# Another order of head pairs, one ScalarE table for exp and log, experts' second products in the scores' banks, tail and first heads laid out anew

## The chip, the core and the metric

The kernel runs on one core of a Trainium2 chip. The core has a TensorE (PE, matmuls; its weight loads are shown apart as PEld), a VectorE (DVE), a ScalarE (ACT), a GpSimd (POOL) and a SyncE (SP), which here only issues DMAs. Each engine works through its own list of instructions in order and waits for others by semaphores. On-chip data lie in SBUF, matmul results in PSUM. The metric is the device time in microseconds (us) of one execution, the median of several runs.

## The reference, cut to what matters

```python
x = layernorm(x + attn1(x)); x = layernorm(x + ffn(x))      # x: (2, 1024, 256) fp32

def attn1(x):                                # one head of width 256, causal, pre-norm
    xn = layernorm(x) * gamma + beta
    q, k, v = xn @ Wq, xn @ Wk, xn @ Wv      # 256 x 256 each
    return softmax(causal(q @ k.T / 16)) @ v @ o_proj + x

def ffn(x):
    a = layernorm(x) * ln1_w + ln1_b
    q, k, v = a @ wq + bq, a @ wk + bk, a @ wv + bv   # 16 heads of 128
    q, k = rope(q), rope(k)
    h = x + (softmax(causal(q @ k.T / sqrt(128))) @ v) @ wo + bo
    t = layernorm(h) * ln2_w + ln2_b
    w = top2_of_4(softmax(t @ w_gate))       # two weights a token, softmax over the two
    m = sum_e w[:, e] * (gelu(t @ we1[e] + be1[e]) @ we2[e] + be2[e])   # all 4 experts computed
    return h + m
```

## The kernel before, in words

All data are fp32. A batch `b` (0 or 1) has 1024 tokens: 8 rows `i` of 128 tokens, in two halves `j` of four rows. The program order is written out by hand: a list `steps` with one step for each row of work (16 rows of the first attention, then 8 rows for each of 32 *units*), and fillers hung on the steps with `at`, `mid`, `end_of`, `first`, `late`. `spread` hands a list of pieces to consecutive steps, so many a step. Step 16 is `A0`; unit number k has the steps 16+8k to 23+8k. Each engine sees its part of this order, so the order decides what waits behind what.

A **unit** is one head of one batch, `(g, b, hh)`: head group `g` (0 to 7) has two heads `hh`, and a *pair* `(g, b)` is two units in a row. `pairs` (L810) sets their order: in the version before, group by group with batch 0 and then 1; the last four pairs run batch 0 of groups 6 and 7, then batch 1 of both.

For each row of a unit (`RowB`): `scores` (L716) multiplies queries and keys into a two-bank PSUM tile `sc` (two such tiles), DVE masks (L329) and takes the negated row maximum (L331), ACT takes exp with the row's sum (L336). What follows has two forms:

- *blocks*: ACT scales the row by 1/sum (L730), DVE transposes it in 32 x 32 blocks (L741) into `pair_sb` (half j=0) or into the space of `x1` (half j=1), and once four rows are there, `gather` (L765) puts the blocks in place by 16 DMAs of the SP queue, in two lots of 8, one step apart. The tile gathered into is `pT`.
- otherwise DVE scales the row (L732), PE transposes it (L348), and ACT and DVE move it to `pT` (L353, L351).

`U0, U1` say which units use blocks: before, from unit 1 on, except the last two units' first halves. `output` (L786) then multiplies `pT` with the values into `av`, so many steps (the *lag*, in `PARTS`) after the half's last row: with the default lags 8 (j=0) and 8, 9, 10 (j=1), given others for the last units; ACT moves `av` to `aT` (L802). When a pair is done, `b_output` (L668, L678) multiplies `aT` with `wo` and adds it to the hidden state `h` (tile `hx`).

Keys, queries and values of the next pair are made while the pair before it runs: `seven_products` (L570 and L561) makes a 2 x 2 block product with seven products and sums of blocks; the sums of weight blocks are `weight_sums` on POOL (L537-L540), those of tokens `x_sums` on DVE (L547, four a batch, once), ACT moves parts (L593, L595), DVE adds (L603). The first two units' keys and queries are made whole, by `b_project` (L506, L513). Each finished 512-column piece of keys or queries is then rotated: two SP DMAs swap its halves into `rot`, which has two buffers (L480, L481), and POOL does three operations (L485-L487, the *rope*), popped from `rope_later` a step later. For the keys of the second pair, DVE did the first of the three (`HELP`). `load_weights` brings a group's weights, from the SP queue if `g` is not 0 and from POOL's if it is; `scale_queries` scales wq on POOL (L472).

PSUM: two score tiles of two banks, two banks `acc` (`acc_tile`, in turn), two banks `tr` for transposes and `av`.

The layernorms take mean and variance by `ln_stats`; 1/std was a Sqrt on ACT and a reciprocal on DVE. exp, Sqrt and Gelu lie in different ACT tables, so between them ACT loads a table (ACT_TABLE_LOAD).

After the attention follow, for each half of each batch: norm (`m_norm`, to `xn`), `m_transposed`, `gate_products`, `gate` and `gate_best` (softmax and the two largest, on DVE with an exp on ACT), `m_bias` (be2 weighted, on DVE, L1177), and for each expert `hidden` (L1190, `acc` banks, Gelu on ACT) and `expert` (L1214, second product; L1223, weighted and added to `h` on DVE). `m_residual` adds `x1`, kept in DRAM meanwhile, on POOL; `o_stats` and `o_finish` normalise and store. The batch-0 part begins beside the last units, which are of batch 1; the rest is a list of calls after the last step (`end` = 272), in which the last half's `output(END)` and the last `b_output` stand too.

Of the kernel before, what the change touches and what calls it, by code (L numbers as in the profile page):

```python
# [12 lines left out]
F32 = mybir.dt.float32  # L13
# [5 lines left out]
P = 128  # L19
# [3 lines left out]
ROPE_THETA = 10000.0  # L23


@with_exitstack
def kernel(
# [117 lines left out]
    eps_t = const.tile([P, 2], F32, name="eps_t")  # L145
    nc.vector.memset(eps_t[:, 0:1], EPS)
    nc.vector.memset(eps_t[:, 1:2], EPS / 4)
    warm = const.tile([P, 1], F32, name="warm")
    nc.scalar.activation(warm, eps_t[:, 0:1], AF.Sqrt)
# [49 lines left out]
    def ln_rstd(var, n, eps):  # L199

        std = small.tile([P, NT], F32, tag="std", name="std")
        nc.scalar.activation(std[:, :n], var, AF.Sqrt, bias=eps)
        rstd = small.tile([P, NT], F32, tag="rstd", name="rstd")
        nc.vector.reciprocal(rstd[:, :n], std[:, :n])
        return rstd

    def ln_apply(dst, src, mean, rstd):
        nc.vector.tensor_scalar(dst, src, mean, rstd, ALU.subtract, ALU.mult)  # L208
# [60 lines left out]
    def a_stats(b, tiles):  # L269
        for k in tiles:  # L270
            ln_stats(mv_x[b], k, x1[:, b * NT + k, :])
        cs = slice(tiles[0], tiles[-1] + 1)
        nc.scalar.activation(
            rstd_x[b][:, cs], mv_x[b][:, cs, 1], AF.Sqrt, bias=eps_t[:, 0:1]
        )

    def a_rstd(b, tiles):
        cs = slice(tiles[0], tiles[-1] + 1)
        nc.vector.reciprocal(rstd_x[b][:, cs], rstd_x[b][:, cs])
# [127 lines left out]
    def a_finish(b, j):  # L407
# [10 lines left out]
        nc.scalar.activation(r, v, AF.Sqrt)  # L418
        rr[b, j] = r

    def a_rfinish(b, j):
        r = rr[b, j]
        nc.vector.reciprocal(r, r)
# [67 lines left out]
    HELP = ("wk",)  # L491
# [172 lines left out]
    def b_output(g, b, tiles):  # L664
# [18 lines left out]
    U0, U1, GP = 1, (NU - 2, NU), 2  # L683
# [4 lines left out]
        (NU - 3, 0): {7: range(0, 4)},  # L688
        (NU - 3, 1): {9: range(0, 8)},
        (NU - 2, 1): {7: range(0, 8)},  # L690
# [5 lines left out]
    class RowB:  # L696
# [36 lines left out]

        def transpose(self):
# [10 lines left out]
            if i % 4 == 0:  # L745
                pTs[self.u, j] = work.tile(
                    [P, 4 * (j + 1), 512], F32, tag=f"pT{j}", name="pT", bufs=1
                )
# [5 lines left out]
        def gather(self, part):  # L754
# [3 lines left out]
            if part == 0:  # L758
                pTs[self.u, j] = work.tile([P, n, 512], F32, tag=f"pT{j}", name="pT", bufs=1)
# [50 lines left out]
    pairs = [(g, b) for g in range(G - 2) for b in range(B)]  # L810
# [29 lines left out]

    ROWS0 = (2, 2, 2, 2, 2, 2, 2, 0)
# [7 lines left out]
    a_rstd(0, J0)  # L849
# [7 lines left out]
    a_rstd(0, J1)  # L857
# [10 lines left out]
    a_rstd(1, ALL)  # L868
# [34 lines left out]
    for k, (name, n) in enumerate((("wk", 0), ("wq", 0), ("wk", 1), ("wq", 1))):  # L903
        at(13 + k // 2, b_project, units[0], name, n)
    at(15, b_value, 0, 0, 0)
# [14 lines left out]
    for r, (name, n) in enumerate((("wk", 0), ("wq", 0), ("wk", 1), ("wq", 1))):  # L920
        at(A0 + 2 + r, b_project, units[1], name, n)
    at(A0 + 6, lambda: weight_sums("wk"))
    at(A0 + 6, lambda: weight_sums("wq"))
    at(A0 + 7, lambda: weight_sums("wv"))
    for n in range(2):
        at(A0 + 7, x_sums, 1, n)
        at(A0 + 8, x_sums, 1, 2 + n)
    for n in range(4):
        at(A0 + 18 + n, x_sums, 0, n)
    for k, (g, b) in enumerate(pairs):  # L930
# [9 lines left out]
        if k + 1 < len(pairs):  # L940
# [3 lines left out]
            if ng != g:  # L944

                before = s0 - NT + (6 if k == 1 else 0)
                at(before, load_weights, ng, ("wk",))
                at(before + (1 if k == 1 else 4), weight_sums, "wk")
# [13 lines left out]
        else:  # L962
            spread(s1, keys + queries, (2, 2, 2, 2, 2, 2, 2, 0))
# [93 lines left out]

    def m_stats(b, tiles):
        for k in tiles:
            ln_stats(mv_h[b], k, h[:, b * NT + k, :])  # L1060

    def m_sqrt(b, tiles):
        cs = slice(tiles[0], tiles[-1] + 1)
        nc.scalar.activation(
            rstd_h[b][:, cs], mv_h[b][:, cs, 1], AF.Sqrt, bias=eps_t[:, 0:1]
        )

    def m_rstd(b, tiles):
        cs = slice(tiles[0], tiles[-1] + 1)
        nc.vector.reciprocal(rstd_h[b][:, cs], rstd_h[b][:, cs])  # L1070

    def m_norm(b, j):

        xn = xn_tile()
        for k in range(4):
            i = 4 * j + k
            ht = h[:, b * NT + i, :]
            ln_apply(xn[:, k, :], ht, mv_h[b][:, i, 0:1], rstd_h[b][:, i : i + 1])
# [45 lines left out]
    def gate(b):  # L1124
# [5 lines left out]
        raw = t3("raw_g")  # L1130
        nc.scalar.activation(raw, lg, AF.Exp)
        raws[b] = raw

    def gate_best(b, n):
# [19 lines left out]
        if n:  # L1154
            e2 = t2("e2")
            nc.vector.tensor_tensor(e2, v, found[b, 0][0], ALU.subtract)
            nc.scalar.activation(e2, e2, AF.Exp)
# [26 lines left out]
    def hidden(b, j, e):  # L1184
        k0 = b * NT + 4 * j
        hT = bpool.tile([P, IC, 512], F32, tag=("Twq", "Twk")[e % 2], name="hT", bufs=BUFS[("wq", "wk")[e % 2]])
        for m in range(IC):
# [10 lines left out]
            nc.scalar.activation(hT[:, m, :], ph, AF.Gelu, bias=par[:, bcol : bcol + 1])  # L1198
        hTs[b, j, e] = hT

    turn, attention_done = [0], []

    def expert(b, j, slots):

        for n0 in range(0, len(slots), 2):
            two = slots[n0 : n0 + 2]
            turn[0] ^= 1
            if turn[0] and attention_done:
# [25 lines left out]
    def o_finish(b, j, ks):  # L1234

        tiles = [4 * j + k for k in ks]
        m_rstd(b, tiles)
        n = len(ks)
        o = xn_tile()
        for k in ks:  # L1240
            i = 4 * j + k
            ln_apply(
                o[:, k - ks[0], :], h[:, b * NT + i, :], mv_h[b][:, i, 0:1], rstd_h[b][:, i : i + 1]
            )
        dst = out[b, ds(tiles[0] * P, n * P), :].rearrange("(n p) d -> p n d", p=P)
        nc.sync.dma_start(dst, o[:, :n, :])
# [3 lines left out]
    at(s, m_stats, 0, J0)  # L1250
    at(s + 2, m_stats, 0, J1)
    at(s + 2, m_sqrt, 0, ALL)
    at(s + 3, m_rstd, 0, ALL)
    at(s + 3, m_norm, 0, 0)
    at(s + 4, m_norm, 0, 1)
    s += NT
# [146 lines left out]
```

## Time and profile before

| | us |
|---|---|
| median of 3 runs (lowest to highest) | 1213.24 (1212.55 to 1214.63) |
| the profiled execution, its time | 1212.0 |
| its span, first to last instruction | 1210.2 |
| PE busy / DVE / ACT / POOL | 1158.6 / 782.1 / 652.0 / 587.1 |
| PE busy in 30 to 60 us, of 30 | 30.00 |
| PE busy in 150 to 200 us, of 50 | 41.65 |
| PE busy in 800 to 1000 us, of 200 | 197.61 |
| PE busy in 1000 to 1150 us, of 150 | 135.91 |
| SP's queue moved | 144.78 MB |

How to read it: busy time is the sum of an engine's instructions, matmul ends are modelled, and PE's rows overlap a little. In rows of single instructions the columns are start, duration, engine, line, operation, output <- inputs, shape and count; "[2.03 <-DVE pr L732]" is the idle time before it and what ended it. In the list of waits the three numbers are the sum, the times and the longest. "clock" is the share of full speed that PE was granted.

### The profile page before, as it was taken

Reading aid. Unit: us, or ns where it says so; the run is one execution under the profiler, and the core shown is the slowest. Engines: PE = TensorE matmul, PEld = TensorE weight load, DVE = VectorE, ACT = ScalarE, POOL = GpSimd, SP = SyncE. Lnnn points to the kernel's source line nnn. Section 1 sums busy time; section 2 is a strip of 40 time slices with the busy share of each in tenths; the row PEclk is TensorE's granted clock in tenths of the full one; section 3 lists DMA queues with packets and bytes.
Section 4 is the critical chain, followed back from the end, with each engine's and each line's share of the span. In section 5 each row is a group of like instructions: output and inputs, shape, how many; then the busy total and the mean of one; then the engine's idle time right before and its main releaser. Section 6 shows DMA issues by size and latency. Waiting matters only on the chain.

```text
span 1210.2 us, 15511 instructions
## 1 busy us (share of the span) xinstructions
PE 1158.6 (96%) x4410; PEld 727.3 (60%) x4410; DVE 782.1 (65%) x1798; ACT 652.0 (54%) x1197; POOL 587.1 (49%) x577
## 2 busy tenths in 40 slices
PE   7999977989999999999999999999999998998997
PEld 5676644565656565666656565756565655655665
DVE  5555767656666666666576666666666667774576
ACT  3344445646565655656565656565655555442423
POOL 4005377655664647474837465665757572003000
PEclk9999999999999999999999999999999999999999
DMA  5001125776666666676666776777767775313001
GB/s 180 1 1 35 61 66 127 166 148 152 162 161 158 156 165 161 145 167 155 159 145 158 167 162 158 168 170 167 171 159 173 171 166 135 79 35 104 18 18 35
DMA packets 239765, 153.81 MB, mean 127 GB/s; under 512 B 20828, under 2 KB 221600, under 8 KB 239168
## 3 DMA queue, kind: packets, MB, share of 16 engines
q1 hardware_dynamic: 236576, 144.78, 51.2%
q0 software_dynamic: 1728, 4.89, 1.3%
q10 hardware_dynamic: 1376, 3.15, 0.7%
q8 instruction: 36, 0.59, 0.2%
q14 instruction: 49, 0.40, 0.1%
HBM read 19.57 MB, written 4.19 MB: 20 GB/s over the span
## 4 chain that ended last, share of the span: by engine, by line
PE 74%; SPq 8%; DVE 7%; DMA 5%; POOL 4%; issue 2%; ACT 1%; POOLq 0%; DVEq 0%; ACTq 0%
PE av L786 18%; PE sc L716 14%; PE pa L570 8%; SPq L765 7%; PE pa L668 6%; PE pa L561 5%; PE pa L1190 4%; PE pc L570 3%; DMA pT<-x 3%; PE sc L370 3%; PE pa L392 2%; PE pc L561 2%; PE pe L1214 1%; PE pa L1214 1%; DVE pair_sb L208 1%
## 5 line engine op out<-in xcount | busy, mean ns | idle before, releaser
L716 PE MATMUL sc<-Twk,Twq 128*128 128x512 f32 (+3 forms) x768 | 290.1, 486 | 0.7 <-POOL Twq L487 0.7
L786 PE MATMUL av<-pT,vg 128*128 128x512 f32 (+3 forms) x768 | 272.1, 493 | 18.7 <-DMA pT<-x 8.8
L730 ACT ACTIVATE pr<-pr,rs 128x640 f32<-128x640 f32 (+1 forms) x240 | 187.7, 782 | 179.4 <-DVE rs L728 179.2
L336 ACT ACTIVATE pr<-sc,nmx 128x128 f32<-128x128 f32 (+7 forms) x272 | 201.0, 739 | 153.4 <-DVE nmx L331 121.0
L786 PEld LDWEIGHTS av<-pT,vg 128*128 128x128 f32 x768 | 143.3, 191 | 140.2 <-issue 102.5
L716 PEld LDWEIGHTS sc<-Twk,Twq 128*128 128x128 f32 x768 | 140.0, 190 | 122.1 <-issue 107.1
L331 DVE TENSOR_REDUCE nmx<-sc 128x1 f32<-128x128 f32 (+7 forms) x272 | 206.1, 758 | 9.4
L329 DVE TENSOR_TENSOR sc<-sc,limit 128x128 f32<-128x128 f32 x272 | 79.6, 293 | 145.0 <-PE sc L716 130.0
L485 POOL TENSOR_TENSOR Twk<-Twk,rope_sb 128x512 f32<-128x512 f32 x60 | 76.4, 1273 | 199.2 <-DMA rot<-Twk 175.7
L486 POOL TENSOR_TENSOR rot<-rot,rope_sb 128x512 f32<-128x512 f32 x128 | 165.5, 1293 | 5.1 <-DMA rot<-Twk 5.1
L741 DVE STREAM_TRANSPOSE x<-pr 128x640 f32<-128x640 f32 (+1 forms) x124 | 128.8, 1039 | 54.4 <-DMA pT<-x 32.0
L668 PE MATMUL pa<-wo_g,aT 128*128 128x256 f32 x512 | 126.5, 380 | 2.1 <-DVE hx L678 1.0
L668 PEld LDWEIGHTS pa<-wo_g,aT 128*128 128x128 f32 x512 | 96.1, 191 | 38.1 <-issue 19.2
L485 POOL TENSOR_TENSOR Twq<-Twq,rope_sb 128x512 f32<-128x512 f32 x64 | 81.5, 1273 | 46.0 <-DMA rot<-Twq 27.3
L487 POOL TENSOR_TENSOR Twk<-Twk,rot 128x512 f32<-128x512 f32 x64 | 81.5, 1273 | 7.4 <-DVE Twk L485 2.5
L487 POOL TENSOR_TENSOR Twq<-Twq,rot 128x512 f32<-128x512 f32 x64 | 81.6, 1276 | 5.0
L678 DVE TENSOR_TENSOR hx<-hx,pa 128x256 f32<-128x256 f32 (+1 forms) x124 | 52.3, 425 | 31.2 <-PE pa L668 29.1
L802 ACT ACTIVATE aT<-av,par 128x512 f32<-128x512 f32 x64 | 43.9, 686 | 46.1 <-PE av L786 46.1
L1190 PE MATMUL pa<-xT,we_sb 128*128 128x512 f32 x128 | 59.4, 603 | 4.8 <-DVE hx L1223 4.8
L595 ACT ACTIVATE part<-pa,par 128x512 f32<-128x512 f32 x62 | 42.6, 687 | 39.5 <-PE pa L570 39.4
L741 DVE STREAM_TRANSPOSE pair_sb<-pr 128x128 f32<-128x128 f32 (+1 forms) x116 | 58.2, 502 | 3.6 <-issue 3.4
L447 POOL TENSOR_TENSOR hx<-x,bo_sb 128x256 f32<-128x256 f32 x16 | 12.2, 763 | 99.5 <-ACT x L444 99.5
(194 smaller groups left out, 1589.5 us busy)
## 6 DMA issues: line engine op xcount, KB each, us to landing
pT<-x SPq DMA_DIRECT2D x496, 128.0 KB, 2.6
pT<-pair_sb SPq DMA_DIRECT2D x464, 64.0 KB, 2.0
rot<-Twk SPq DMA_DIRECT2D x128, 128.0 KB, 2.3
rot<-Twq SPq DMA_DIRECT2D x128, 128.0 KB, 2.4
wk_g<-in_L_ffn_wk_dram SPq DMA_DIRECT2D x9, 256.0 KB, 3.1
wq_g<-in_L_ffn_wq_dram SPq DMA_DIRECT2D x9, 256.0 KB, 3.2
wv_g<-in_L_ffn_wv_dram SPq DMA_DIRECT2D x9, 256.0 KB, 3.0
wo_g<-in_L_ffn_wo_dram SPq DMA_DIRECT2D x9, 256.0 KB, 2.9
```

Source lines behind the costliest of these rows:

```text
L331: nc.vector.tensor_reduce(nmx, sc[:, :L], AX.X, ALU.max, negate=True)
L336: nc.scalar.activation(pr[:, :L], sc[:, :L], AF.Exp, bias=nmx, accum_out=sm)
L485: eng.tensor_tensor(t[:, cs], t[:, cs], rope_sb[:, 0, cs], ALU.mult)
L486: nc.gpsimd.tensor_tensor(rot, rot, rope_sb[:, 1, cs], ALU.mult)
L487: nc.gpsimd.tensor_tensor(t[:, cs], t[:, cs], rot, ALU.add)
L570: nc.tensor.matmul(pa, lhsT=w, rhs=x, start=start, stop=True, skip_group_check=True)
L668: nc.tensor.matmul(pa[:, ts(k, D)], lhsT=aT[g, b][:, hh, ts(i, P)], rhs=wg["wo"][:, hh, :], start=(hh == 0), stop=(hh == GH - 1),)
L716: nc.tensor.matmul(sc[:, ds(n0, n)], lhsT=qT[:, ts(i, P)], rhs=kT[:, ds(n0, n)], start=True, stop=True,)
L730: nc.scalar.activation(self.pr[:, :L], self.pr[:, :L], AF.Copy, scale=rs)
L741: nc.vector.transpose(z[:, i % 4, :n, :], self.pr[:, : n * 32].rearrange("p (m s) -> p m s", s=32))
L786: nc.tensor.matmul(cut(av), lhsT=vg[g, b][:, c, ts(hh, HD)], rhs=cut(pT[:, c, :]), start=(c == 0), stop=(c == i),)
L1190: nc.tensor.matmul(ph, lhsT=we1_sb[:, e, c, ts(m, P)], rhs=x2T[:, c, ds(k0 * P, 512)], start=(c == 0), stop=(c == DC - 1),)
```

## The change

The diff makes these edits:

1. Order of pairs: `(0,0), (1,0), (1,1), (0,1)`, then groups 2 to 5 with both batches each, then the last four as before. Group 0's weights are loaded a second time.
2. First heads: unit 1's keys and queries at steps 15 and 16 (were 18 to 21); the second pair's keys in unit 0 from its row 3 on, its queries in unit 1, one each step; group 1's weights and sums accordingly; `x_sums` of batch 0 at steps 14, 14, 15, 19 and of batch 1 at 24 to 27 (were batch 1 at 23 and 24, batch 0 at 34 to 37). `HELP` is empty.
3. One table: `ln_rstd` takes 1/std as exp(-0.5 ln(var)) on ACT; `TABLE`, which holds both, is loaded at the start, and again by `table()` before such an operation when a Gelu has been between. The reciprocals go.
4. Tail of attention: unit 30's first half uses blocks; units 29 and 30 use the default lags or 8 and 9; the last unit's first `pT` lies in a `vg` buffer. Batch 0's norm runs on POOL into free key and query buffers; statistics, norm, transposes, gate products and gate stand at other steps.
5. Experts: `expert` with four slots puts all four results in one score tile; with two slots it takes a score tile or an `acc` bank in turn.
6. After the last step: another order of calls; `o_finish` normalises on ACT (Identity with scale and bias) and stores from the ACT queue.

```diff
-    HELP = ("wk",)
+    HELP = ()
+    def ln_rstd(rstd, var, eps=0.0):
+        nc.scalar.activation(rstd, var, AF.Ln, bias=eps)
+        nc.scalar.activation(rstd, rstd, AF.Exp, scale=-0.5)
...
-    U0, U1, GP = 1, (NU - 2, NU), 2
+    U0, U1, GP = 1, (NU - 1, NU), 2
     PARTS = {
...
-        (NU - 3, 0): {7: range(0, 4)},
-        (NU - 3, 1): {9: range(0, 8)},
-        (NU - 2, 1): {7: range(0, 8)},
+        (NU - 2, 1): {8: range(0, 4), 9: range(4, 8)},
         (NU - 1, 0): {4: range(0, 4)},
         (NU - 1, 1): {END: range(0, 8)},
...
-    pairs = [(g, b) for g in range(G - 2) for b in range(B)]
+    pairs = [(0, 0), (1, 0), (1, 1), (0, 1)]
+    pairs += [(g, b) for g in range(2, G - 2) for b in range(B)]
     pairs += [(g, b) for b in range(B) for g in (G - 2, G - 1)]
...
+    XS0 = (14, 14, 15, A0 + 3)
+    XS1 = (A0 + 8, A0 + 9, A0 + 10, A0 + 11)
...
+    for k, (name, n) in enumerate((("wk", 0), ("wk", 1), ("wq", 0), ("wq", 1))):
+        at(A0 - 1 + k // 2, b_project, units[1], name, n)
-    for r, (name, n) in enumerate((("wk", 0), ("wq", 0), ("wk", 1), ("wq", 1))):
-        at(A0 + 2 + r, b_project, units[1], name, n)
...
-                before = s0 - NT + (6 if k == 1 else 0)
+                before = s0 - NT if k else s0
                 at(before, load_weights, ng, ("wk",))
-                at(before + (1 if k == 1 else 4), weight_sums, "wk")
+                at(before + (4 if k else 3), weight_sums, "wk")
...
-            spread(s1, keys + queries, (2, 2, 2, 2, 2, 2, 2, 0))
+            spread(s0, keys, (0, 0, 0, 1, 1, 2, 2, 1))
+            spread(s1, queries, (1, 1, 1, 1, 1, 1, 1, 0))
...
+    def table():
+        if other:
+            nc.scalar.preload_act_table_set(TABLE)
+            other.clear()
...
+    def m_norm(b, j, eng=nc.gpsimd):
+        if b:
+            xn = xn_tile()
+        else:
+            xn = bpool.tile([P, 4, D], F32, tag=("Twk", "Twq")[j], name="xn", bufs=BUFS[("wk", "wq")[j]])
...
-        for n0 in range(0, len(slots), 2):
-            two = slots[n0 : n0 + 2]
-            turn[0] ^= 1
-            if turn[0] and attention_done:
+        for n0 in range(0, len(slots), 4):
+            two = slots[n0 : n0 + 4]
+            if len(two) > 2 or slots[0][1] % 2:
                 pe = ps_sc.tile([P, S], F32, tag="sc", name="pe")
             else:
                 pe = acc_tile()
...
+        nc.vector.scalar_tensor_tensor(
+            nb[:, :n], mv_h[b][:, cs, 0], -1.0, rstd_h[b][:, cs], ALU.mult, ALU.mult
+        )
...
+            nc.scalar.activation(
+                o[:, n0, :], h[:, b * NT + i, :], AF.Identity,
+                bias=nb[:, n0 : n0 + 1], scale=rstd_h[b][:, i : i + 1],
+            )
...
-        nc.sync.dma_start(dst, o[:, :n, :])
+        nc.scalar.dma_start(dst, o[:, :n, :])
```

The steps of the tail, counted from unit 30's first (256), before and after: statistics 0 and 2 in both; norm 3 and 4, now 1 and 3; transposes 4 to 7, now 5 to 8; gate products 6 to 9, now 9, 9, 10, 11; first `hidden` 6, now 8; `gate` 9, now 11; `gate_best` 10 and 11, now 11 and 12; `gate_weights` 12, now 13. After the last step the order of batch 0's second half and batch 1's preparation is now:

```diff
     all_of(0, 0, 2)
+    hidden(0, 1, 0)
+    gate_products(1, (0, 1))
+    gate_products(1, (2, 3))
+    all_of(0, 0, 3)
     steps[end - 1][0].output(END)
-    hidden(0, 1, 0)
+    m_bias(0, (6, 7))
+    hidden(0, 1, 1)
     for i in (4, 6):
         b_output(G - 1, 1, (i, i + 1))
...
     m_stats(1, J1)
...
+    all_of(0, 1, 0)
+    o_stats(0, 0, J0)
+    hidden(0, 1, 2)
+    m_rstd(1, J1)
+    m_rstd(0, J0)
+    m_norm(1, 1, nc.vector)
+    all_of(0, 1, 1)
+    m_residual(1, J1)
     for c in range(DC):
         m_transposed(1, 1, c)
```

Batch 1's first norm and its transposes stand before `all_of(0, 0, 2)`.

## The prediction

> **What bounds the kernel now.** I read the shares of the page first, then the busy time by stretch, then TensorE's (PE's) waits, then single rows around each wait.
>
> ```profile
> span 1210.2 us, 15511 instructions
> PE 1158.6 (96%) x4410; PEld 727.3 (60%) x4410; DVE 782.1 (65%) x1798; ACT 652.0 (54%) x1197; POOL 587.1 (49%) x577
> ```
>
> ```profile
> 60.00:90.00 30.00, 30.00 (x145) 23.07 (x144) 15.54 (x46) 14.24 (x28) 2.17 (x3) 1.00 0.00 1
> ...
> 150.00:200.00 50.00, 41.65 (x158) 22.98 (x156) 36.21 (x68) 28.36 (x55) 36.98 (x36) 1.00 0.30 79
> ...
> 600.00:800.00 200.00, 199.96 (x769) 123.72 (x768) 133.94 (x290) 122.96 (x232) 112.54 (x104) 1.00 0.68 158
> ...
> 1100.00:1125.00 25.00, 21.67 (x83) 14.29 (x82) 11.97 (x26) 9.14 (x11) 11.41 (x16) 0.93 0.08 35
> ```
>
> The columns are stretch, length, then busy time of PE, PEld, DVE, ACT and POOL, granted clock, DMA share, GB/s. PE is the bound: in the middle (600 to 800 us) it idles 0.04 us in 200, so nothing done there to DVE, ACT or POOL can bring time. What can be won is PE's 51.6 us of idle (1210.2 - 1158.6) and some clock, and both lie at the ends:
>
> ```profile
> PE av L786 <- DMA pT<-x: 8.8, 6, 3.7
> PE av L786 <- DMA pT<-pair_sb: 8.0, 3, 4.1
> PE pt L348 <- DVE pr L732: 5.4, 3, 2.5
> ...
> PE pa L1190 <- DVE hx L1223: 4.8, 3, 2.0
> ```
>
> Idle by place, from PE's rows: start 6.8; **A**, 143 to 169 us, 9.4 (2.03+0.85+0.68+0.26+1.49+2.52+1.55); **B**, 193 to 208, 6.5 (0.70+1.69+4.11); **C**, at 255, 3.7; changes of head group at 310 to 600, some 2.6; **D**, last attention rows, 930 to 1025, 6.6 (0.50+0.57+1.31+3.31+0.87); **E**, 1049 and 1071, 2.0 (1.04+0.96); **F**, experts, 7.8 (1.52+1.64+0.48+0.40+0.40+2.02+1.30); after the last matmul 6.1. A long wait costs twice, since the matmuls behind it run slowly:
>
> ```profile
> 207.61 4.08 PE L786 MATMUL av<-pT,vg 128*128 128x512 f32 x8 [4.11 <-DMA pT<-pair_sb]
> ...
> 230.70 2.32 PE L786 MATMUL av<-pT,vg 128*128 128x512 f32 x8
> ```
>
> The same eight matmuls take 4.08 us after the wait, 2.32 without it. The granted clock is 0.83 over 207 to 217, 0.94 and 0.89 over 247 to 267, 0.97 and 0.86 over 1110 to 1130: 1.7 us each behind B, C and F (shortfall times 10 us).
>
> **Order of pairs and first heads (A, B, C).** Unit 1's projections move from steps 18-21 to 15-16, the next pair's keys from unit 1 to unit 0, its queries stay in unit 1, one each step. PE's work is the same. POOL's ropes (3 x 1.27 us a tile) start where POOL now idles 12.0 us (127 to 139.5), so its queue at 190 to 197 goes. That queue makes B:
>
> ```profile
> 195.85 1.27 POOL L487 TENSOR_TENSOR Twq<-Twq,rot 128x512 f32<-128x512 f32 x1
> ...
> 197.12 0.53 SPq L480 DMA_DIRECT2D rot<-Twq  x1
> ...
> 200.20 5.59 SPq L765 DMA_DIRECT2D pT<-pair_sb  x8
> ```
>
> SP's next rotation waits for one of two rot buffers, which POOL frees at 197.1; the second half of unit 1's gather is queued behind it and lands as PE continues at 207.6. Afterwards unit 1 carries 4 tiles' rotations (8 DMAs) instead of 8 (16), and the wk and wq loads leave SP's queue there too: SP saves 8 x 0.57 + 2 x 0.53 = 5.6 us, more than the 4.11. The wait for ACT's part (1.69), itself behind late DVE rows, I keep at 0.7. B: 6.5 + 1.7 - 0.7 = **-7.5** (0 to -8.2).
>
> A is DVE: 9.83 busy of 10 us in 140 to 150 and 160 to 170. It loses four x_sums of batch 1 (1.61+1.64+0.78+0.94 = 5.0) and a reciprocal (0.2), gains one x_sum of batch 0 (0.68 to 1.61, take 1.0) and net two key sums (1.4): -2.8. With fewer ropes beside it the rest shortens too (two L208 take 2.78 us there, four take 1.38 at 14.6 us). The two normalising applies and row sums stay. Ends 0 and -9.4; I take **-5**.
>
> C stays: the gather of unit 2 shares the DMA engines with the 1 MB we1 load (step 40, landing 9.3 us), and in the compiled order POOL issues group 0's wk just ahead of it instead of wv on SP. **0** (+3 to -5.4).
>
> The order 0,1,1,0,2 loads group 0 a second time: four DMAs, which go through POOL because g is 0. Behind each on POOL queue the ropes, behind these SP's rotations and gathers; each waits until PE has read the old tile. Here a rule speaks against the change. The row: the first four such loads took 0.70 to 0.72 us of POOL each, with DVE working, and landed in 6.1 to 6.2 us, against 2.9 to 3.2 through SP. The Trainium skill, "SBUF — State Buffer", the box on DVE blocking DMA, says that a POOL-issued DMA cannot write its descriptors while DVE holds the shared port: about 3.1 us instead of 0.62. By the row the loads cost POOL 2.9 us over four units, by the rule 12.4. POOL idles about 12 us of a 28 us unit (44% in 600 to 800), so either is hidden; I take the row, and **+0.7** for one more change of group (a wait of 0.84 us at 371, behind a pT<-x gather; ends 0 and 3).
>
> **One table.** The page and the compiled order give 30 table loads before and 18 after; Sqrt plus DVE reciprocal becomes Ln plus Exp (0.30 us each, as the Sqrt).
>
> ```profile
> L1198 ACT ACT_TABLE_LOAD x9 | 11.5, 1283 | 14.0 <-PE pa L1190 13.9
> L336 ACT ACT_TABLE_LOAD x8 | 10.3, 1283 | 8.2 <-DVE nmx L331 6.0 <-DVE lg L1108 2.1
> L1064 ACT ACT_TABLE_LOAD x6 | 7.7, 1283 | 0.1
> ```
>
> By the row that is 12 x 1.28 = 15.4 us of ACT. The Trainium skill, "ScalarE: Activation LUTs", What ACT_TABLE_LOAD costs, adds a drain of 1.38 us and gives 2.66: 31.9 us. In this trace an exp ends at 1137.92, the load starts at 1137.94 and the next Gelu at 1139.23: no drain shows, and I take 1.28. Of either sum almost nothing is on the path, for ACT is 54% busy: at 137.5 to 140.8 two loads delay an exp while DVE is busy anyway. **0** of its own.
>
> **Tail.** D: batch 0's norm goes to POOL and to tiles of its own (8 x about 0.75, half of L472's 1.49 for 512 columns), two steps ahead of its transposes, while POOL idles from 1004 on. So pair_sb is free for the gathers of unit 30's first half: 16 more gathers on SP (10.5 us, no rotations are left then), and 10 PE transposes fewer at 0.107 (eight take 0.86): **-1.1**. Unit 29's first half is read at lag 8 instead of 7, about 3 us later, against a wait of 3.31. Of D's 6.6 the 2.4 of 936, 965 and 995 stay, and of the rest I leave 1.2: **-3.0** (+1 to -6).
>
> E: the output products now follow four more av matmuls (2.15 us), which hide ACT's aT (0.96 goes). But gate and its first best stand in one step, with a table load (1.28) and exp between them on ACT: DVE waits some 2 us, then the hidden-state adds, then PE. I take +1.3: **+0.3** (-1 to +3).
>
> F: experts' second products leave the two acc banks to hidden, and take two score tiles of two banks. The waits of 1.52, 2.02 and 1.30 were hidden's first product behind L1223 on a DVE busy with m_bias (4.0 us) or L208 (5.1). Unit 31's last av, now some 10 us later, gives its gather (landing 1095.4) time; batch 1's second norm has 10 us of products before its transposes. Late next is DVE itself (four L1223 take 1.7 us of 6.9 a round) and ACT in a round with two table loads, Ln, Exp and four Identity (0.61 each, the L444 row): 2.6+0.6+2.4+1.4 = 7.0 us against 6.9. I leave 1.5 of 7.8 + 1.7: **-8.0** (+2 to -9.5).
>
> End: DVE loses reciprocal and apply (0.54 a tile), so the last L1223, which starts 0.8 behind PE's end (1204.1) now, starts 0.4 earlier; ACT then has Ln, Exp, one tile's Identity and its DMA issue (0.4) before the last Identity, 2.1 us instead of 1.0: **+0.7**.
>
> Sum: -7.5 - 5 + 0 + 0.7 + 0 - 1.1 - 3.0 + 0.3 - 8.0 + 0.7 = -22.9. The profiled execution took 1212.0 us (span 1210.2 and 1.8 around it): 1189.1. The median of the runs is 1.2 above it, so **1190**.
>
> **Rivals.**
> 1. *Tail only moves its waits* (DVE and ACT late in F, POOL late in D): D, E and F bring nothing, 1190 + 11 = 1201. For it: ACT's 7.0 against 6.9. Against: the freed banks. 0.14.
> 2. *First heads stay bound by DVE and SP*: A and B bring nothing, 1190 + 12.5 = 1202. For it: A's applies stay. Against: POOL's idle 12 us. 0.12.
> 3. *More goes*: C (5.4) and the rest of A (4.4) too: 1180. 0.17.
> 4. *The change does little*: new waits eat all, 1212. 0.03.
> 5. *Slower: POOL's queue.* A group 0 load blocks POOL until PE has passed and the ropes behind it miss their step. Each time SP's gather is late as in B: 4.11 + 1.7 = 5.8 us, four times 23.2, and C grows by 3: 1216. It decides from a POOL delay above its 12 us of slack a unit. 0.05.
>
> The forecast itself, 1184 to 1197: 0.49. A measurement of this kernel tells 0.2% from nothing, 1210.8 to 1215.7. Range **1179 to 1203**, rivals 1 to 3 mostly inside. Faster 0.92, same 0.03, slower 0.05.
>
> **What would show it.** B right: no PE wait on pT<-pair_sb near 200 us and a clock near 1.00 there. A: DVE below 9 of 10 us at 140 to 170. C: a PE wait on pT<-x of 3 to 4 us near 245. F: no PE wait on L1223, clock 1.00 to the last matmul. E: a wait on L678 of over 1 us beside gate. Wrong: POOL waiting on PE at its weight loads, or PE idle in 250 to 450.

## The result, and the profile after

The changed kernel takes 1197.2 us (median of 4 runs, 1195.82 to 1197.69) against 1212.99 for the kernel before on the same chip (4 runs, 1212.55 to 1214.63). The ratio is 0.9866, with a 95% interval of 0.9848 to 0.9883. The profiled execution took 1197.6 us with a span of 1195.8. The forecast was 1190 with a range of 1179 to 1203: the sign and the range held. Profile to profile (1212.0 to 1197.6) the saving was 14.4 us, where the sum had 22.9.

The first lines of the page after:

```profile
span 1195.8 us, 15503 instructions
...
PE 1153.4 (96%) x4400; PEld 725.9 (61%) x4400; DVE 768.7 (64%) x1760; ACT 649.8 (54%) x1221; POOL 607.1 (51%) x594
```

PE's idle time went from 51.6 us to 42.4. The busy time by stretch (length, then PE, PEld, DVE, ACT, POOL, granted clock, DMA share, GB/s) for the places A, B, C, D and F of the prediction:

```profile
140.00:150.00 10.00, 8.56 (x38) 5.72 (x38) 6.86 (x19) 3.60 (x11) 3.21 (x6) 1.00 0.00 0
160.00:170.00 10.00, 8.69 (x43) 5.22 (x42) 7.82 (x15) 6.23 (x13) 8.75 (x8) 1.00 0.33 76
200.00:210.00 10.00, 7.53 (x30) 4.36 (x29) 4.09 (x11) 4.54 (x9) 1.48 (x2) 1.00 0.75 172
250.00:260.00 10.00, 10.00 (x44) 6.83 (x43) 5.95 (x13) 4.82 (x8) 8.26 (x8) 0.83 0.49 117
1020.00:1030.00 10.00, 9.29 (x23) 4.53 (x24) 5.61 (x11) 5.56 (x9) 0.00 (x0) 0.83 0.30 72
1120.00:1130.00 10.00, 9.19 (x45) 6.61 (x45) 5.84 (x20) 4.95 (x6) 2.50 (x4) 1.00 0.00 0
```

DVE is below 9 of 10 us in both stretches of A (it was 9.83 in each). The clock is 1.00 behind B and F. It is still 0.83 behind C, and it is now 0.83 in 1020 to 1030, where it was 1.00. PE's rows with the waits that remain:

```profile
149.73 0.52 PE L338 MATMUL pt<-ident,pr 128*128 128x128 f32 x3 [1.44 <-DVE pr L719]
...
172.43 5.83 PE L777 MATMUL av<-pT,vg 128*128 128x512 f32 x16 [1.21 <-DVE rs L715]
...
197.54 1.13 PE L550 MATMUL pc<-S,xT 128*128 128x128 f32 x8 [1.72 <-ACT part L582]
...
202.94 2.39 PE L777 MATMUL av<-pT,vg 128*128 128x512 f32 x8 [2.47 <-DMA pT<-pair_sb]
...
249.01 2.81 PE L777 MATMUL av<-pT,vg 128*128 128x512 f32 x4 [3.58 <-DMA rot<-Twq]
...
932.12 1.95 PE L777 MATMUL av<-pT,vg 128*128 128x512 f32 x4 [1.73 <-DMA rot<-Twq]
...
1003.74 2.40 PE L777 MATMUL av<-pT,vg 128*128 128x512 f32 x8 [0.65 <-DMA pT<-pair_sb]
...
1020.71 3.10 PE L777 MATMUL av<-pT,vg 128*128 128x512 f32 x4 [4.61 <-DMA pT<-pair_sb]
...
1120.55 0.33 PE L210 MATMUL pt<-ident,pair_sb 128*128 128x128 f32 x1 [0.41 <-DVE pair_sb L204]
```

At 249.01 and 932.12 the profile names a rotation; the same reads in b_lag and d_swap wait for their gathers (pT<-x). The row at 1020.71 is new: 4.61 us of idling, and the four matmuls behind it take 3.10 us where four take 1.88 at full clock (row 1020.59 of the run d_gather below). The places in one table, PE's idle time and lost clock together, against the prediction's terms:

| place | before | after | change | forecast |
|---|---|---|---|---|
| A, 120 to 187 us | 9.4 | 5.8 | -3.6 | -5 |
| B, 189 to 208 | 8.2 | 5.2 | -3.0 | -7.5 |
| C, near 250 | 5.4 | 5.3 | -0.1 | 0 |
| changes of group | 2.6 | 3.0 | +0.4 | +0.7 |
| **D**, 930 to 1025 | 6.6 | 10.6 | **+4.0** | **-3.0** |
| E | 2.0 | 1.4 | -0.6 | +0.3 |
| F, experts | 9.5 | 0.8 | -8.7 | -8.0 |
| PE transposes saved | | | -1.1 | -1.1 |
| after the last matmul | 6.1 | 6.5 | +0.4 | +0.7 |

These add up to -12.3. The other 2.1 us of the 14.4 lie in PE's busy time and in no place that I could name: it fell by 5.2 us, of which the saved transposes and the clock make 2.8. Of D's +4.0, 1.2 is the wait at 932 (0.50 before, 1.73 now); in the runs below that leave this place alone it lies between under 0.25 (d_late) and 1.49 (d_load), so it may be chance. The table (edit 3) has no place of its own, and has a run of its own below.

### The profile page after: what moved, and what is told of

Same layout as the page of the kernel before. It is cut to its first block, busy times and chain, and to the rows that moved or that the text cites. A ratio compares the mean times of both kernels' runs of the same rounds, so it can differ in the third digit from the quotient of the medians.

```text
span 1195.8 us, 15503 instructions
## 1 busy us (share of the span) xinstructions
PE 1153.4 (96%) x4400; PEld 725.9 (61%) x4400; DVE 768.7 (64%) x1760; ACT 649.8 (54%) x1221; POOL 607.1 (51%) x594
## 4 chain that ended last, share of the span: by engine, by line
PE 76%; SPq 7%; POOL 5%; DMA 5%; DVE 4%; issue 2%; ACT 1%; POOLq 0%; ACTq 0%; DVEq 0%
PE av L777 18%; PE sc L703 14%; PE pa L559 8%; PE pa L657 6%; SPq L756 6%; PE pa L550 5%; PE pa L1187 5%; PE pe L1210 4%; PE pc L559 3%; PE sc L360 3%; PE pa L382 2%; PE pc L550 2%; POOL rot L475 2%; DMA rot<-Twq 1%; POOL Twk L476 1%
## 5 line engine op out<-in xcount | busy, mean ns | idle before, releaser
L474 POOL TENSOR_TENSOR Twk<-Twk,rope_sb 128x512 f32<-128x512 f32 x64 | 82.0, 1280 | 201.2 <-DMA rot<-Twk 154.9
L657 PEld LDWEIGHTS pa<-wo_g,aT 128*128 128x128 f32 x512 | 96.3, 191 | 35.2 <-issue 18.5
L1079 POOL TENSOR_TENSOR hx<-hx,x 128x256 f32<-128x256 f32 x16 | 12.7, 827 | 96.8 <-DVE hx L1219 84.6
```

The source lines that it names most:

```text
L474: eng.tensor_tensor(t[:, cs], t[:, cs], rope_sb[:, 0, cs], ALU.mult)
L657: nc.tensor.matmul(pa[:, ts(k, D)], lhsT=aT[g, b][:, hh, ts(i, P)], rhs=wg["wo"][:, hh, :], start=(hh == 0), stop=(hh == GH - 1),)
```

## The experiments

Each kernel ran on the same chip as the kernel before, which took 1214.7 to 1215.1 us there (median), so ratios are compared, not times. Runs of one kernel lay up to 9 us apart, and the ratios' intervals are 0.2 to 0.9% wide. What a part is worth is therefore read from its place in the profile first, and from the ratio second. One of the runs (d_late) left D, and all before it, as in the changed kernel, and got 0.9849 against that kernel's 0.9866: ratios that differ by this little are not told apart. Of the runs that alter the changed kernel, only best is told apart from it by the ratio.

### D: who makes unit 29's second half late?

The new wait is for the second half of unit 29. SP's queue there (start, time taken by all, line, operation, how many):

```profile
1002.57 11.28 SPq L756 DMA_DIRECT2D pT<-x  x16
1013.96 12.46 SPq L756 DMA_DIRECT2D pT<-pair_sb  x16
```

The first row is unit 29's gather, the second the new one of unit 30. In the same stretch POOL loads 768 KB (issued at 1011.7 and 1012.5 us), and PE reads from lag 8 on, not at 9. The suspects were these three, and a fourth, that PE had lost work ahead of the read.

**d_lag**

```diff
     PARTS = {
...
+        (NU - 3, 1): {9: range(0, 8)},
         (NU - 2, 1): {8: range(0, 4), 9: range(4, 8)},
```

> The changed kernel with one row of the read plan put back: the second half of unit 29 is read whole at lag 9 again, not in parts from lag 8. Theory 1, the lag: TensorE simply asks a step too early, and the wait of 4.61 us at 1020.7 us shrinks by the work of a step in between (a pair of transposes 0.9 us, scores 0.5, about 1.5 in all)[...]: 1194 to 1196 us instead of 1197. Theory 2, the loads (768 KB of expert weights and biases beside the gather): the gather lands as late as before, the wait shrinks by 1.5 at most and the clock still falls: 1195.5. Theory 3, the 16 new gathers of unit 30: like theory 2. A drop to 1191 or below would say that the lag alone was the fault.

Ratio 0.9861 (0.9829 to 0.9892). The wait did not shrink; it became 6.56 us, and the clock was 0.66 in 1020 to 1030. Rows of this run near the end of the wait:

```profile
1022.96 0.85 DVE L735 STREAM_TRANSPOSE x<-pr 128x640 f32<-128x640 f32 x1 [5.67 <-DMA pT<-pair_sb]
...
1023.94 0.93 ACT L718 ACTIVATE pr<-pr,rs 128x768 f32<-128x768 f32 x1 [5.44 <-DVE rs L716]
...
1024.78 0.76 ACT L215 ACTIVATE xT<-pt,par 128x512 f32<-128x512 f32 x1
...
1025.59 1.22 PE L778 MATMUL av<-pT,vg 128*128 128x512 f32 x1 [6.56 <-DMA pT<-pair_sb]
```

DVE waits for the same landing, since unit 30 transposes into the space that unit 29's gather still reads. ACT waits for DVE, and ACT's next piece, behind that, empties the transpose bank that `av` needs. PE starts as that piece ends (1024.78 + 0.76 = 1025.54). So a later read is held by this chain instead: the lag is not the cause.

The landing itself shows in this first DVE row after the gather. In the changed kernel, d_swap and d_gather:

```profile
1020.68 0.84 DVE L734 STREAM_TRANSPOSE x<-pr 128x640 f32<-128x640 f32 x1 [5.03 <-DMA pT<-pair_sb]
```

```profile
1019.59 0.84 DVE L735 STREAM_TRANSPOSE x<-pr 128x640 f32<-128x640 f32 x1 [3.99 <-DMA pT<-x]
```

```profile
1019.90 0.84 DVE L734 STREAM_TRANSPOSE x<-pr 128x640 f32<-128x640 f32 x1 [2.83 <-DMA pT<-x]
```

All times of the next table count from SP's first issue of unit 29's gather. "PE ready" is the start of PE's read less its wait; the wait is the landing less this time, where it comes later. The runs b_keys, c_split, f_banks and b_lag, which come further below, leave D as in the changed kernel.

| run | unit 30's 16 gathers beside it | POOL's 768 KB issued | landing | PE ready | wait of PE |
|---|---|---|---|---|---|
| changed kernel | yes | 9.1 | 1020.68 - 1002.57 = 18.1 | 13.5 | 4.61 |
| b_keys, c_split, f_banks, b_lag | yes | 9.1 | 16.9, 17.6, 17.9, 18.5 | 13.5 to 13.6 | 3.36, 4.14, 4.38, 5.00 |
| d_late | yes | 9.1 | 1018.62 - 1000.40 = 18.2 | 13.5 | 4.72 |
| d_load | yes | 9.1 | 1022.52 - 1005.01 = 17.5 | 13.5 | 4.00 |
| d_swap | no | 9.1 | 1019.59 - 1002.50 = 17.1 | 13.5 | 3.57 |
| d_gather | no | 10.5 | 1019.90 - 1003.62 = 16.3 | 17.0 | none |
| best (last run) | no | 10.5 | 1012.21 - 996.80 = 15.4 | 17.0 | none |

With nothing changed at D the landing lies anywhere from 16.9 to 18.5 and the wait from 3.36 to 5.00. PE is ready at the same time in all of them but d_gather and best, which keep unit 30's first half on PE's transposes.

**d_load**

```diff
-    at(A0 + 30 * NT + 6, load_second, (3,))
+    at(A0 + 31 * NT + 1, load_second, (3,))
```

> The changed kernel with the load of the last expert's second weights and of the biases (256 and 512 KB) three steps later, behind both gathers. Theory 1, the lag: the wait of 4.61 us stays, 1197 us. Theory 2, the loads: the last gather of unit 29 lands some 3.5 us earlier (768 KB at about 200 GB/s are 3.8 us), the wait falls to 0.5 to 1.5 us and the clock loss of 1.7 us goes: 1192 us. Theory 3, the new gathers: the landing moves by less than 1 us, 1196 to 1197.

Ratio 0.9857 (0.9826 to 0.9887). This edit did not part the loads from the gather. POOL's first load in the changed kernel and in d_load:

```profile
1011.68 0.77 POOL L1021 DMA_DIRECT2D lent<-in_L_ffn_we_dram  x1
```

```profile
1014.15 0.77 POOL L1021 DMA_DIRECT2D lent<-in_L_ffn_we_dram  x1
```

Both come 9.1 us after the gather's first issue (1002.57 and 1005.01): on POOL they follow the norm of batch 0 with nothing in between, so three steps later in program order is no later there. The wait of 4.00 is within the spread of the table. What the loads cost at D was therefore not tried, and stays open.

**d_gather**

```diff
-    U0, U1, GP = 1, (NU - 1, NU), 2
+    U0, U1, GP = 1, (NU - 2, NU), 2
```

> The changed kernel with the first half of unit 30 back on TensorE's transposes, so without its 16 gathers; the loads and the lag stay as changed. TensorE gets 10 transposes more (1.1 us). Theory 1, the lag: the wait stays near 4.6 less what the added transposes fill, 1197. Theory 2, the loads: the gather of unit 29 still shares the DMA engines with 768 KB, its landing moves by less than 1 us, wait about 3.5 to 4.5, 1197 to 1198. Theory 3, the new gathers: without the 1 MB beside it the gather lands 3 us or more earlier, wait under 1.5 and no clock loss: 1193 to 1194 in spite of the transposes.

Ratio 0.9841 (0.9813 to 0.9868). The wait is gone. PE's rows there:

```profile
1016.17 2.42 PE L777 MATMUL av<-pT,vg 128*128 128x512 f32 x8 [0.56 <-ACT pT L343]
1018.43 0.60 PE L210 MATMUL pt<-ident,xn 128*128 128x128 f32 x4
1018.87 1.88 PE L703 MATMUL sc<-Twk,Twq 128*128 128x512 f32 x4
1020.59 1.88 PE L777 MATMUL av<-pT,vg 128*128 128x512 f32 x4
```

The read at 1020.59 does not wait. The landing came 1.8 us earlier, and PE is ready 3.4 us later (17.0 instead of 13.5). The second is the first row: with PE's own transposes, unit 30's first half is read at lag 3, so its eight matmuls (2.2 us, and 1.1 us of transposes before them) stand ahead of unit 29's read. With the gathers they stand behind it, at lag 8.

**d_late and d_swap** were to part these two: hold back unit 30's gathers and leave PE's order alone. d_late issues them two steps later in program order and reads them a step later (lag 9).

```diff
+                late29 = steps[t - 4 - k][0] if is_blocks(t - 4 - k) else None
+                if late29 and late29.u == units[NU - 2] and late29.i == 3:
+                    late29.gather(k)
```

> The changed kernel with unit 30's 16 gathers of its first half issued two steps later (behind the read of unit 29's second half instead of beside its gather) and read at lag 9 instead of 8. TensorE's work and its order up to that read stay as changed, so this tells what the gathers share from what TensorE lost as cover. If the 16 gathers delay unit 29's gather on the DMA engines: its landing comes 2 us earlier after its first issue (16 us instead of 18), the wait of 4.6 us falls to about 2.5, and the clock loss of 1.7 us goes: 3 to 4 us faster than the changed kernel. If the lost cover alone (1.1 us of transposes and 2.4 us of products that stood ahead of the read) is the cause: the wait stays above 4 and the time within 1 us of the changed kernel's.

It changed nothing (ratio 0.9849, 0.9827 to 0.9872). SP's queue in d_late and then in d_swap:

```profile
1000.40 11.24 SPq L757 DMA_DIRECT2D pT<-x  x16
1011.75 12.58 SPq L757 DMA_DIRECT2D pT<-pair_sb  x16
```

```profile
1002.50 11.71 SPq L757 DMA_DIRECT2D pT<-x  x16
1028.22 10.26 SPq L757 DMA_DIRECT2D pT<-pair_sb  x16
```

SP's own order is the same in d_late, and a later place among the other engines' steps delayed nothing here, where SP has no wait. d_swap gives it one, by a buffer that is not free before:

```diff
-            if self.u == units[-1] and j == 0:
+            if self.u == units[-2] and j == 0:
                 return bpool.tile(shape, F32, tag="vg", name="pT")
...
+        (NU - 3, 1): {8: range(0, 8)},
```

> The changed kernel with two buffers exchanged: unit 30's first half goes into the value tile's buffer, which is free only when TensorE has read unit 29's second half, and unit 31's first half into the one of its own; unit 29's second half is read in one piece at lag 8. So unit 30's 16 gathers cannot start beside unit 29's (the run d_late only moved them in program order, and SP, which had nothing else to do, issued them at the same moment). TensorE's order ahead of the read is as in the changed kernel. If the gathers share the DMA engines with unit 29's: its landing comes 16 us after its first issue instead of 18, and the wait of 4.6 us falls to about 2.5 with no clock loss behind it. If the lost cover alone is the cause: the wait stays above 4. In both cases a later wait for unit 30's own gather may come.

Ratio 0.9846 (0.983 to 0.9863). PE's read in d_swap:

```profile
1019.61 8.57 PE L778 MATMUL av<-pT,vg 128*128 128x512 f32 x16 [3.57 <-DMA pT<-x]
```

The wait is 3.57 and the clock still falls (0.74 in 1020 to 1030), with unit 30's gathers gone from beside unit 29's. So these gathers are not the main cause: the wait is within the spread of the runs that have them. What d_gather has and d_swap has not is PE's work ahead of the read. This cover is 3.4 of the 4.61 us. The other 1.2 went because the landing came 1.8 us earlier. Whether this is the DMA engines no longer shared with unit 30's gathers or the loads that POOL issued 1.4 us later there, these runs do not tell.

### C and B: the load of 1 MB, and what a gain at B is worth

**c_split**

```diff
-        nc.gpsimd.dma_start(
-            we1_sb.rearrange("p e c i -> p (e c) i"), we1.rearrange("e (c p) i -> p (e c) i", p=P)
-        )
+    def load_first(e):
+        nc.gpsimd.dma_start(we1_sb[:, e], we1[e].rearrange("(c p) i -> p c i", p=P))
...
-    at(A0 + 3 * NT, load_experts)
+    at(A0 + 8 * NT + 1, load_experts)
+    for e in range(E):
+        at(A0 + (8 + 2 * e) * NT + 1, load_first, e)
```

> The changed kernel with the 1 MB load of the experts' first weights cut into four loads of 256 KB, each at the start of another pair of heads between 490 and 720 us, where the DMA engines are half idle. If this load is what makes the gather of unit 2 late (the wait of 3.58 us at 249.0 us and the 1.7 us of clock behind it), both go and nothing comes in their place: 1192 us. If the reload of group 0's keys at the same step, or SP's queue alone, does it: the wait stays above 2 us, 1196 to 1197. If the four small loads disturb other gathers: new waits of 1 us at 490 to 720 us.

Ratio 0.9828 (0.9785 to 0.9872), span 1192.0. SP's queue ahead of C, in the changed kernel and in c_split:

```profile
229.70 1.74 SPq L470 DMA_DIRECT2D rot<-Twq  x1
231.55 7.64 SPq L756 DMA_DIRECT2D pT<-x  x8
...
240.70 5.29 SPq L756 DMA_DIRECT2D pT<-x  x8
```

```profile
228.94 0.60 SPq L470 DMA_DIRECT2D rot<-Twq  x1
229.65 6.13 SPq L756 DMA_DIRECT2D pT<-x  x8
...
237.13 5.28 SPq L756 DMA_DIRECT2D pT<-x  x8
```

Without the load beside it, the second lot of unit 2's gather starts 8.2 us after the rotation of the first row and not 11.0, PE does not wait near 250, and the clock stays at 1.00 there. In the runs that leave C alone the wait lies between 3.48 (b_keys) and 5.07 us (f_banks), so its absence is no chance. The next wait is 0.52 us at 260. The Trainium skill, "DMA: Bandwidth & Descriptors", section "Issuing engines are not separate DMA queues", says that DMAs of all issuing engines run on the same 16 DMA engines and interleave. These rows agree: with a load issued by POOL beside them, SP's own issues took longer (7.64 us for eight against 6.13). The four small loads cost nothing that shows: PE's waits between 280 and 920 us add up to 2.8 us in c_split and 3.0 in the changed kernel.

**b_lag and b_keys.** b_lag reads unit 1's first half a step later. b_keys moves the last four key products of the next pair back into unit 1.

```diff
+        (U0, 0): {9: range(0, 4)},
```

```diff
-            spread(s0, keys, (0, 0, 0, 1, 1, 2, 2, 1))
-            spread(s1, queries, (1, 1, 1, 1, 1, 1, 1, 0))
+            spread(s0, keys[:3], (0, 0, 0, 1, 1, 1, 0, 0))
+            spread(s1, keys[3:] + queries, (2, 2, 2, 2, 1, 1, 1, 0))
```

> The changed kernel with one row added to the read plan: unit 1's first half is read at lag 9 instead of 8. SP issues the 16 gathers of unit 1 and one rotation back to back from 187.8 to 201.1 us, so the landing at 202.9 us cannot move. If TensorE merely comes too early, because unit 1 lost the key products (7 x 0.86 us) that stood there before, the step between (scores 1.0, value products 2 x 0.9) covers the wait of 2.5 us: 1 to 2.5 us faster. If VectorE, which waits for the same landing before its next transpose into pair_sb, holds the scores behind it, the wait only changes its name: within 0.5 us.

> The changed kernel with the last four of the seven key products of the next pair moved back from unit 0 to the start of unit 1, where they stood before: 4 x 0.86 = 3.4 us of TensorE's work ahead of unit 1's read, and 3 rotations (6 DMAs, 3.4 us on SP) with it. If what is left of the wait at 203 us is lost cover, it falls from 2.5 to under 1 us and the time by 1 to 2 us, unless unit 0, now emptier, waits more on VectorE. If it is the length of SP's queue, as the forecast had it, the wait grows to 4 us or more and the clock falls behind it: 2 to 4 us slower than the changed kernel.

b_lag: ratio 0.9854 (0.9824 to 0.9883). b_keys: 0.9882 (0.9864 to 0.9901). PE's rows in b_lag, then in b_keys:

```profile
196.93 1.13 PE L550 MATMUL pc<-S,xT 128*128 128x128 f32 x8 [1.72 <-ACT part L582]
...
249.64 3.75 PE L778 MATMUL av<-pT,vg 128*128 128x512 f32 x4 [7.04 <-DMA pT<-x]
```

```profile
204.19 4.61 PE L777 MATMUL av<-pT,vg 128*128 128x512 f32 x8 [4.94 <-DMA pT<-pair_sb]
```

In b_lag the wait at 203 us is gone, and C's wait is 7.04 us instead of 3.58: PE comes to the gather of unit 2 earlier (at 242.6 instead of 245.4), and this lands no earlier (249.6, 249.0). All of B's gain is given back 45 us later. In b_keys the wait at B is 4.94 us, longer than the 4.11 of the kernel before, with a clock of 0.66 in 200 to 210. Counted from the end of DVE's transpose of unit 1's fourth row, the gather lands 18.2 us later in the kernel before, 15.6 in the changed one and 18.2 in b_keys, where two rotations of SP stand ahead of it again. PE is ready for it after 13.3 us in both of the last two. So the prediction's mechanism at B is confirmed (rotations in SP's queue ahead of the gather), and the key products are no cover for this read.

### F and the table: which part brought it

**f_banks** puts the old banks into the changed kernel, **banks_only** the new banks into the kernel before.

```diff
-        for n0 in range(0, len(slots), 4):
-            two = slots[n0 : n0 + 4]
-            if len(two) > 2 or slots[0][1] % 2:
+        for n0 in range(0, len(slots), 2):
+            two = slots[n0 : n0 + 2]
+            turn[0] ^= 1
+            if turn[0] and attention_done:
```

> The changed kernel with the experts' second products back on two-slot tiles that alternate between the accumulation banks and the score tiles, as before; the new order of the tail stays. If the banks are what freed the hidden products (forecast: most of the 8 us of step F), waits of hidden's first product on VectorE come back, 4 us or more in all, with 1 to 2 us of clock: 4 to 8 us slower than the changed kernel. If the new order of the tail does it (the norm of batch 1 and the bias additions spread out), the time stays within 2 us.

> The kernel before with the experts' second products in the scores' banks alone, four slots a tile; order of the tail, table and heads as before. The changed kernel with the old banks kept all but 0.9 us of step F's gain. If the banks and the new order of the tail each are enough, the waits of hidden's first product (1.5, 1.6, 2.0 and 1.3 us) go here too, with the 1.7 us of clock: 5 to 8 us faster than before. If the order alone does it, the waits stay: within 2 us of before.

f_banks: ratio 0.9869 (0.9847 to 0.989). banks_only: 0.9974 (0.9963 to 0.9985, 20 runs), or 3.2 us faster than before. PE's rows of F with the waits that differ, in f_banks and then in banks_only:

```profile
1131.81 1.98 PE L1187 MATMUL pa<-xT,we_sb 128*128 128x512 f32 x4 [0.48 <-DVE hx L1222]
...
1156.60 1.99 PE L1213 MATMUL pa<-lent,hT 128*128 128x256 f32 x8 [0.42 <-ACT hT L1195]
```

```profile
1094.95 5.24 PE L786 MATMUL av<-pT,vg 128*128 128x512 f32 x8 [3.48 <-DMA pT<-x]
...
1122.30 1.05 PE L1100 MATMUL pg<-wgate_sb,xT 128*128 128x4 f32 x8 [0.57 <-ACT xT L219]
```

With the old banks the new order loses 0.9 us. With the new banks alone the three waits on L1223 (1.52, 2.02, 1.30) go, but PE then comes earlier to the last unit's gather and waits 3.48 us there instead of 1.64, and the clock loss stays (0.83 in 1090 to 1100 and in 1110 to 1120). So either the banks or the order takes away the waits on L1223. Only the order, which moves the last unit's read some 10 us back, takes away the wait for its gather too.

**table_only** is the kernel before with edit 3 alone.

```diff
-        nc.scalar.activation(r, v, AF.Sqrt)
+        ln_rstd(r, v)
...
-        nc.vector.reciprocal(rstd_h[b][:, cs], rstd_h[b][:, cs])
+        table()
+        ln_rstd(rstd_h[b][:, cs], mv_h[b][:, cs, 1], eps_t[:, 0:1])
```

> The kernel before with the one ScalarE table alone: Ln and Exp in the place of Sqrt and VectorE's reciprocal, and the table named ahead of them; all else as before. By the forecast (12 loads of 1.28 us fewer on an engine that is 54% busy and hardly on the path): 0, at most 1 us faster. If the loads cost the path[...]: some us faster, up to 10. If the added Exp comes in ScalarE's way: up to 2 us slower.

Ratio 0.9953 (0.9934 to 0.9971), 3.5 to 8 us. Its places in the profile show little of this: A is 8.9 instead of 9.4 (DVE 8.90 busy in 160 to 170 where it was 9.83), F 7.6 instead of 7.8. Most of the rest is clock: the granted clock is 0.9946 in the mean of its five runs and 0.9918 in that of the 24 of the kernel before beside them, by estimate 0.0028 x 1210 = 3.4 us. The interval lies clear of the forecast's 0; whether the table is what kept the clock up stays open.

### The three repairs together

**best** is the changed kernel with d_gather, c_split and b_lag.

> The changed kernel with the three edits that belong together: unit 30's first half on TensorE's transposes again (D), the experts' first weights in four loads at quiet places (C), and unit 1's first half read at lag 9 (B). Each by itself: D about 5 us less by its place in the profile, C about 5, B 0 because C's wait grew by as much. If the three add up, B's 2 us stay now that C's wait is gone: 1185 to 1188 us, 0.976 to 0.979 of before. If PE's earlier arrival opens a wait for unit 2's gather again: 1188 to 1190.

1189.24 us against 1214.68; ratio 0.9789 (0.9768 to 0.981). Its page and its places B and D:

```profile
span 1186.7 us, 15506 instructions
...
PE 1151.2 (97%) x4410; PEld 725.4 (61%) x4410; DVE 769.4 (65%) x1760; ACT 648.3 (55%) x1221; POOL 608.5 (51%) x597
```

```profile
200.00:210.00 10.00, 10.00 (x35) 5.70 (x35) 6.05 (x16) 6.29 (x12) 1.18 (x1) 1.00 0.77 176
...
1020.00:1030.00 10.00, 9.74 (x49) 7.19 (x47) 3.58 (x10) 5.94 (x8) 0.00 (x0) 1.00 0.01 2
```

```profile
244.29 1.96 PE L778 MATMUL av<-pT,vg 128*128 128x512 f32 x4 [1.45 <-DMA pT<-x]
```

At C 1.45 us of wait is left, since PE arrives earlier, and no clock is lost. The span is 9.1 us below that of the changed kernel's profile and 23.5 below that of before's. The intervals of the ratios do not overlap, so this version beats both; what each of the three repairs brings of it is not told by the ratios (0.9841, 0.9828 and 0.9854 alone, 0.9866 without). About half of the 9 us is clock, by estimate: it is 0.9985 in the mean of these four runs and 0.9940 in that of the changed kernel's four, and 0.0045 x 1190 = 5.4 us.

## Why the prediction was right, and where it was not

- **Sign, bound and range**: right. PE was the bound, its idle time lay at the ends, and the change moved that. The range of 24 us was wide enough to hold a miss of 7.0 us at D and one of 4.5 at B, both to the same side.
- **F** (-8.0, measured -8.7): the size is right and the main reason only half. The prediction leaned on the freed banks; f_banks gets all but 0.9 us without them. Either the banks or the order is enough for the waits on L1223. Only the order, with the last read behind other work, which the prediction named as its second reason, takes away the wait for the last gather too.
- **D** (-3.0, measured +4.0) is **the step that failed**: "Of D's 6.6 the 2.4 of 936, 965 and 995 stay, and of the rest I leave 1.2". The wait that it looked at, unit 29's first half, did go (3.31 to 0.65). It counted the 16 new gathers as SP time and the 10 transposes as PE time saved, and did not ask what the removed PE work had covered: unit 30's transposes and products would stand ahead of unit 29's second half. Without them PE reaches that read early, and DVE waits for the same landing. The runs put 3.4 us of the 4.61 on lost cover and leave open what made up the other 1.2; 1.7 of clock come on top.
- **B** (-7.5, measured -3.0): right mechanism, too large. The prediction set 5.6 us of issues, saved over the whole of unit 1, against the wait of 4.11. Ahead of the landing only 2.6 were saved (18.2 to 15.6 us after the fourth row), of which 1.8 between the two lots of the gather, and PE was ready 0.8 earlier too (14.1 to 13.3). SP needs 13 us for the 16 gathers and one rotation alone:

```profile
187.84 6.68 SPq L756 DMA_DIRECT2D pT<-pair_sb  x8
...
195.88 5.18 SPq L756 DMA_DIRECT2D pT<-pair_sb  x8
```

  So 2.47 us are left. The wait for ACT's part, of which the sum left 0.7, stayed whole (1.69, now 1.72). And of the 3.0 that came, 1.7 is clock and in part luck: the same first heads lost it in three other runs (c_split, d_lag and d_swap, 0.83 in 200 to 210). b_lag shows that a gain at B is worth nothing while C stands behind it.
- **The clock**: "A long wait costs twice" does not hold for each long wait, so the 1.7 us behind B and F were no sure gain. The same eight matmuls of unit 29's first half behind the same wait, in the kernel before and in table_only:

```profile
1008.22 2.39 PE L786 MATMUL av<-pT,vg 128*128 128x512 f32 x8 [3.31 <-DMA pT<-pair_sb]
```

```profile
1006.21 4.09 PE L779 MATMUL av<-pT,vg 128*128 128x512 f32 x8 [3.31 <-DMA pT<-pair_sb]
```

- **A** (-5, measured -3.6): right in kind; unit 1's projections brought two small waits of their own (0.67 and 0.34 at 124 to 126).
- **C** (0): right, and the cause named there, the 1 MB load, is shown by c_split.
- **Group 0 by POOL** (+0.7, measured +0.4): right; no PE wait on these loads, which took POOL 0.73 to 0.76 us each, near the row that the prediction went by. Rival 5 fell.
- **One table** (0): too low by the ratio of table_only; how much of that is the table's is open.
- **The end** (+0.7, measured +0.4): near. **E** (+0.3, measured -0.6): small, but of the other sign. The wait on L678 beside gate did not come; a wait of 1.14 us on ACT's exp came at 1057.

## What to carry to other kernels

When work is taken off the bounding engine, ask which transfer it was covering, and add that wait to the sum; at D this was worth more than the work saved. Look for the next transfer that ends at a fixed time: a gain ahead of it only moves the wait, as at B, until that transfer is repaired too. A large load beside a queue of many small gathers is cheap only where nobody waits for these gathers soon; cut it up and put the pieces elsewhere.

## What the runs showed of the hardware that was not expected

- POOL's normalising operation (128x256, two per-row scalars) takes 1.22 us, against 0.41 to 0.62 for the same on DVE; the prediction had estimated 0.75. In this place it was hidden.
- An issue that was put later in the program was not later on its queue where nothing held that queue: in d_late SP's 16 gathers followed the earlier ones by 0.1 us, as before, and in d_load POOL's loads came 9.1 us after the gather's first issue, as before.
- Waits of the same length cost clock or not: behind 3.31 us the clock was 1.00 in 1000 to 1020 in the kernel before and 0.83 in 1000 to 1010 in table_only; at B it was 0.83 in 200 to 210 behind 2.08 us (c_split) and 2.35 us (d_swap), and 1.00 behind 2.47 us in the changed kernel. What decides it was not tried.
- The clock also fell without a long wait. In d_gather it is 0.74 in 1032 to 1034 and 0.50 in 1034 to 1036, although PE's longest wait since 1016.2 is 0.26 us; what runs there just before are gate products of 4 columns. That these are the cause was not tried.
